# Moving copies, additions and one division between engines in a fused attention and FFN kernel

## The chip, the cores and the metric

The kernel runs on one core of one Trainium2 chip, as one launch. The metric is the device time of the program in microseconds (us). Its engines are named as the profile names them: PE is TensorE (matrix products and transposes), DVE is VectorE, ACT is ScalarE, POOL is GpSimd, SP is SyncE (here only DMA issue). Each engine works through its own queue in order, and waits on semaphores for the others.

## The reference

`x` is 2 x 2048 rows of 512, f32; the encoder output `enc` is 2 x 128 rows of 512. There are 16 heads of width 32, and 128 keys.

```python
q = layernorm(x) @ wq + bq;  k = enc @ wk + bk;  v = enc @ wv + bv
score = q k^T / sqrt(32) * mask           # per head
score = where(score == 0, -1e9, score)
context = softmax(score) @ v              # over 128 keys
x = x + context @ wo + bo
n = layernorm(x)
y = real(ifft(fft(n) @ (w_re + i w_im)))  # over the 512 columns
out = x + y + bias
```

## The kernel before

The 4096 rows are cut into 8 groups of four tiles of 128 rows. Tile (i, t) is tile t of group i. Everything that belongs to one group is spread over about three groups of time: while the softmax of group i runs, the queries of group i+1 are made, the rows of group i+2 are normalized and transposed, and the output projection and the FFN of group i-1 run.

**Softmax of a tile.** `begin` (L760) lets PE make the scores of 16 heads (32 products, L326) into two PSUM tiles of two banks each, one for each half of the heads. Each half then goes through four steps. `masked` (L345, DVE) multiplies scores by the mask and puts them into SBUF. `maxima` (L352, L354, L355, all DVE) marks zeros, takes the row maxima of 8 heads and scales them. `exponentials` (L361, ACT) is 8 ACTIVATE instructions with a sum each. `divided` is a reciprocal on DVE (L373) and a multiplication by it, on GpSimd unless another engine is given (L374).

**Transposed weights.** `transposed_weights(i, t, first, end, eng, banks)` (L380) lets PE transpose the divided weights of four heads into one PSUM bank (L399), once for each g from first to end, and copies each bank to SBUF (tensor `pt`), on ACT (L390) or on the engine `eng` (L388). Four such copies, g = 0 to 3, make up a tile. With `banks`, all transposes come first and go into the banks given.

**PSUM.** There are eight banks: two tiles of two banks for scores (`ps_sc`, tag sc), two single banks for transposes (`ps_tp`, tag tp) and two for matrix chains (`ps_mm`, tag mm). In each pool the buffers are used in turn: a third request waits until the first one has been read out. `transpose_rows` (L185) transposes four 128 x 128 blocks (L194) and copies them out (L196 on ACT, L198 otherwise); its argument `spare` picks the pool. `chain` (L204) is four accumulating products (L210), in the mm pool or, with `spare=True`, in the tp pool. Both a chain of queries (`Queries`), of the projection (`Project`) and of the FFN (`Ffn`) has a `pe` and an `evict` part, and `between` puts transposes in the middle of a chain.

**Other helpers.** `relative` (L234) subtracts its first column from a tile of rows: one instruction on DVE or GpSimd (L244), two on ACT (L241, L242). `query_statistics` and `query_norm` (L227) normalize it; `query_transposes` transposes it (tensor `xnT`, on ACT). `output_bias` (L435) adds `bo` to the four residual tiles of a group, on GpSimd (L439), before `Project.evict` (L460) adds the projection. `ffn_statistics`, `ffn_norm` (L227 on DVE, then the FFN's bias on GpSimd, L479) and `ffn_transposes` prepare the FFN; `Ffn.evict` (L524) adds and stores. `Mirrored` and `First` make the 512 x 512 matrix of the FFN (`m_ffn`) out of its Fourier weights, during group 0.

**Order.** The kernel is built under a manual schedule: the order of the calls is the order of each engine's queue. Group 0 and the first two tiles of group 1 (L880 to L1027) are written out by hand, as are tiles 1 to 3 of the last group (L1144 on). In between, `slot` (L765) places the work of one tile: its hooks `pool`, `early`, `mid_a`, `on_a`, `on_m`, `mid_b`, `mid_c`, `on_b`, `end` and `on_c` take extra calls, and `carried` holds calls put off to the next slot, where they run right after the first `masked`. `turned` names the tile whose weights are transposed in the slot, which is the tile before.

Of the kernel before, what the change touches and what calls it, by code (L numbers as in the profile page):

```python
# [14 lines left out]
P = 128  # L15
# [7 lines left out]
def kernel(  # L23
# [210 lines left out]
    def relative(i, t, eng):  # L234


        xt = rows[i][t]
        d = work.tile([P, D], FP, tag="rel", bufs=4, name=f"rel_{i}_{t}")
        if eng is nc.scalar:
            less = small.tile([P, 1], FP, tag="less", name=f"less_{i}_{t}")  # L240
            nc.scalar.mul(less, xt[:, 0:1], -1.0)  # L241
            nc.scalar.activation(d, xt, AF.Identity, bias=less)  # L242
        else:
            eng.tensor_scalar(d, xt, xt[:, 0:1], None, ALU.subtract)  # L244
        rels.setdefault(i, []).append(d)
# [39 lines left out]
    class Queries:  # L285


        def __init__(self, i, g, first=0, spare=False):
            self.i, self.g, self.first, self.spare = i, g, first, spare
# [87 lines left out]

    pts = {}

    def transposed_weights(i, t, first, end, eng=None, banks=None):  # L380
        if t == 0 and first == 0:
            pts[i] = [big_tile("pt", 6, f"pt_{i}_{g}") for g in range(NC)]
        ws = weights[i, t]

        def copy(g, ps):
            dst = pts[i][g][:, :, t * P : (t + 1) * P]
            if eng:
                eng.tensor_copy(dst, ps)  # L388
            else:
                nc.scalar.copy(dst, ps)  # L390

        for g in range(first, end):
            ps = (
                banks[g]
                if banks
                else ps_tp.tile([P, NR, P], FP, tag="tp", name=f"tpw_{i}_{t}_{g}")
            )
            for r in range(NR):
                nc.tensor.transpose(  # L399
                    ps[:, r, :], ws[r // 2].w[:, (r % 2) * NC + g, :], ident  # L400
                )
            if not banks:
                copy(g, ps)
        if banks:
            for g in range(first, end):
                copy(g, banks[g])

# [24 lines left out]
            else:  # L432
                eng.tensor_copy(cT[:, g, :], ps)

    def output_bias(i):  # L435

        xs = groups[i]
        for t in range(TG):
            nc.gpsimd.tensor_tensor(xs[:, t, :], xs[:, t, :], bo, ALU.add)  # L439

    fstats = {}
# [42 lines left out]
        transpose_rows(nTs[i, t], norms.pop((i, t)), f"f{i}_{t}", eng, spare)  # L484

    class Ffn:
        def __init__(self, i, t):
            self.i, self.t = i, t

        def pe(self, between=()):  # L490
            nT = nTs.pop((self.i, self.t))
            self.ps = chain(
                f"y_{self.i}_{self.t}",
                lambda c: nT[:, c, :],
                lambda c: m_ffn[:, c, :],
                between=between,
            )

        def in_halves(self):
# [208 lines left out]
    def load_first_rows(name, pieces):  # L708

        rows = small.tile([NC, P], FP, tag="rows0", bufs=2, name=name)  # L710
        for k, piece in enumerate(pieces):
            nc.sync.dma_start(rows[k : k + 1, :], piece)
        return rows
# [242 lines left out]
    h[1].first()  # L956
    w[0].exponentials()
    w[1].masked()
    transposed_weights(0, 2, 0, HC, nc.vector)
    h[1].second()  # L960
    h[2].pe()
    h[2].evict()
# [3 lines left out]
    h[3].first()  # L966
    w[1].maxima()
    w[0].divided()
    relative(3, 0, nc.gpsimd)
    h[2].second()  # L970
    h[3].second()
    load_residual(0)
    rows_m = load_first_rows("rows_m", [x.lhs(HC)[0:1, :] for x in m])
    w[1].exponentials()
    run(q[0])
    transposed_weights(0, 2, HC, NC, nc.vector)
    w[1].divided()
    relative(3, 1, nc.gpsimd)

    load_mask(2)  # L980
    w = begin(1, 0)
# [1 line left out]
    m[0].pe()  # L983
    add = first_rows("add_m", rows_m)
    m[0].evict(add[:, 0:1])
    w[0].maxima()
    relative(3, 2, nc.gpsimd)
    relative(3, 3, nc.gpsimd)
    m[1].pe()
    m[1].evict(add[:, 1:2])  # L990
    transposed_weights(0, 3, 0, HC)
    w[0].exponentials()
    w[1].masked()
    w[1].maxima()
# [13 lines left out]
    context(0, 0, NC, nc.scalar, True)  # L1008
    m[3].pe()
    m[3].evict(add[:, 3:4])  # L1010
    output_bias(0)
    w[0].maxima()
    q[2].pe()
    w[0].exponentials()
    w[1].masked()
    q[2].evict()
    free = ps_sc.tile([P, 2, NC, K], FP, tag="sc", name="tpw_1_0")
    transposed_weights(1, 0, 0, HC, nc.vector, [free[:, g] for g in range(HC)])
    transposed_weights(1, 0, HC, NC)
    w[1].maxima()  # L1020
    q[3].pe()
# [2 lines left out]
    query_norm(3, 0)  # L1024
    query_norm(3, 1)
    w[0].divided()
    carried.append(w[1].divided)  # L1027


    for i in range(1, last - 1):  # L1030
        p, pp, n, nn = i - 1, i - 2, i + 1, i + 2
        q = [Queries(n, g) for g in range(NC)]
        q_nn = Queries(nn, 0)
        o = [Project(p, t) for t in range(TG)]
        f_p = Ffn(p, 0)
        if i > 1:
            load_rows(nn)
            load_mask(n)
            load_residual(p)
            f_pp = [Ffn(pp, t) for t in range(TG)]  # L1040
            slot(
                i,
                0,
                [f_pp[1], f_pp[2], q[1]],
                turned=(p, TG - 1),
                early=[(ffn_transposes, pp, 2)],
                pool=[(relative, nn, t, nc.gpsimd) for t in range(TG)],
                on_b=[(ffn_norm, pp, 3), (query_statistics, nn, 0, 2)],
                on_c=[(query_statistics, nn, 2, TG)],
            )  # L1050
            slot(
                i,
                1,
                [q[2], q[3], f_pp[3]],
                turned=(i, 0),
                early=[(context, p, 0, NC, nc.scalar, True), (ffn_transposes, pp, 3)],
                pool=[(output_bias, p)],
                on_b=[(query_norm, nn, 0), (query_norm, nn, 1)],
            )
        slot(  # L1060
            i,
            2,
            o[:3],
            turned=(i, 1),
            early=[(query_transposes, nn, 0), (query_transposes, nn, 1)],
            on_a=[(ffn_statistics, p, 0)],
            on_m=[(ffn_norm, p, 0), (query_norm, nn, 2), (query_norm, nn, 3)],
            on_c=[(ffn_statistics, p, 1)],
            end=[(ffn_transposes, p, 0)],
        )  # L1070
        slot(
            i,
            3,
            [o[3], f_p, q_nn],
            turned=(i, 2),
            early=[(query_transposes, nn, 2), (query_transposes, nn, 3)],
            on_a=[(ffn_statistics, p, 2)],
            on_b=[(ffn_norm, p, 1), (ffn_statistics, p, 3)],
            on_c=[(ffn_norm, p, 2)],
            end=[(ffn_transposes, p, 1)],  # L1080
        )
# [41 lines left out]
        pool=[(ffn_norm, p, 0)],  # L1123
        mid_a=[(ffn_transposes, p, 0, nc.scalar, ps_sc)],
        on_a=[(ffn_statistics, p, 1)],
        on_b=[(ffn_norm, p, 1), (ffn_statistics, p, 2), (ffn_statistics, p, 3)],
        end=[(ffn_transposes, p, 1)],
    )
    i, p, pp = last, last - 1, last - 2
    o = [Project(p, t) for t in range(TG)]  # L1130
    f = f_p
    f_p = [Ffn(p, t) for t in range(TG)]
    slot(
        i,
# [60 lines left out]
    w[0].exponentials()  # L1195
    w[1].masked()
    f_p[0].evict()
    f_p[1].pe(between=[(ffn_transposes, p, 2, nc.vector)])
    ffn_norm(p, 3)
    w[1].maxima()  # L1200
    transposed_weights(i, 2, HC, NC)
# [79 lines left out]
```

## Time and profile before

| | |
|---|---|
| median of 3 runs | 530.56 us (530.26 to 532.3) |
| the profiled execution | 530.73 us, of which the instructions span 528.6 |
| PE busy | 519.5 us, 98% |
| DVE busy | 433.5 us, 82% |
| ACT busy | 339.0 us, 64% |
| POOL busy | 335.0 us, 63% |
| PE clock granted | full speed |

The profile is one execution, taken by the hardware profiler. Its first part gives each engine's busy time with its share of the span. Rows of waits name who waited for whom, with the total, the count and the longest wait in us. The chain that ended last is followed back from the last instruction, at each step to what released it. Rows of a timeline give start, duration, engine, line, operation, output and input, shapes, and a count where equal neighbours are merged; in square brackets stands the idle time before, with what ended it. Releasers are inferred from semaphores. L12 is line 12 of the kernel before.

### The profile page before, as it was taken

The numbers are of one execution on the slowest core, as the hardware profiler recorded it, in microseconds if no ns is written. First come the engines' busy times: TensorE is split into PE (matmuls) and PEld (weight loads), VectorE is DVE, ScalarE is ACT, GpSimd is POOL, SyncE is SP. The second block draws the span as 40 slices with busy tenths as digits, with TensorE's granted clock in tenths as the row PEclk, the third lists the DMA queues.
The fourth block names the chain that finished last, engine by engine and source line by source line (L and its number), as shares of the span: only waits on it lengthen the run. The fifth ranks groups of instructions, "written<-read, shape, count | busy, mean of one in ns | idle before, by whom it ended". The sixth has DMA issues, their size and how long they took to land.

```text
span 528.6 us, 8816 instructions
## 1 busy us (share of the span) xinstructions
PE 519.5 (98%) x3028; PEld 294.8 (56%) x3028; DVE 433.5 (82%) x618; ACT 339.0 (64%) x1290; POOL 335.0 (63%) x275
## 2 busy tenths in 40 slices
PE   8999999989999999999999999999999999999997
PEld 7756675545545555455545555455545555455444
DVE  4789898989887988889887998889876898998351
ACT  3367878486667776666677676666686677766210
POOL 2779379955993559635894459635764466756450
PEclk9999999999999999999999999999999999999999
DMA  8962030000600033000610015000312001201002
GB/s 317 383 236 79 1 100 3 0 2 0 221 21 20 1 115 125 1 20 1 200 41 1 20 60 180 1 22 0 120 42 65 35 1 61 100 0 52 29 0 81
DMA packets 22892, 36.49 MB, mean 69 GB/s; under 512 B 2104, under 2 KB 7488, under 8 KB 22848
## 3 DMA queue, kind: packets, MB, share of 16 engines
q1 hardware_dynamic: 22160, 34.75, 19.1%
q10 hardware_dynamic: 688, 1.18, 0.6%
q8 instruction: 24, 0.39, 0.3%
q14 instruction: 20, 0.16, 0.1%
HBM read 27.53 MB, written 8.39 MB: 68 GB/s over the span
## 4 chain that ended last, share of the span: by engine, by line
PE 77%; DVE 14%; ACT 5%; POOL 1%; issue 1%; DMA 1%; SPq 0%; ACTq 0%; POOLq 0%; DVEq 0%
PE q L210 17%; PE y L210 16%; PE o L210 16%; PE tpw L399 8%; PE sc L326 5%; PE c L423 5%; ACT w L361 4%; DVE w L352 3%; DVE nmax L354 3%; PE tp_a L194 3%; DVE w L345 3%; PE tp_f L194 2%; PE k L568 1%; PE v L210 1%; DVE norm_f L227 1%
## 5 line engine op out<-in xcount | busy, mean ns | idle before, releaser
L361 ACT ACTIVATE w<-w,nmax 128x128 f32<-128x128 f32 x512 | 198.3, 395 | 21.0 <-DVE nmax L355 17.0
L374 POOL TENSOR_TENSOR w<-w,rden 128x1024 f32<-128x1024 f32 x62 | 118.8, 1920 | 71.7 <-DVE rden L373 56.3
L210 PE MATMUL o<-wo,cT 128*128 128x512 f32 x256 | 115.3, 594 | 0.0
L210 PE MATMUL y<-m_ffn,nT 128*128 128x512 f32 x248 | 112.1, 594 | 0.5 <-DVE x L524 0.5
L210 PE MATMUL q<-xnT,wq 128*128 128x512 f32 (+1 forms) x256 | 111.6, 580 | 0.0
L361 ACT ACTIVATION_READ_ACCUMULATOR w<-w,nmax 128x1 f32 x512 | 99.3, 194 | 0.0
L390 ACT COPY pt<-tpw 128x512 f32<-128x512 f32 x114 | 60.9, 586 | 55.6 <-PE tpw L399 55.4
L352 DVE SCALAR_TENSOR_TENSOR w<-w 128x1024 f32<-128x1024 f32 x64 | 87.9, 1373 | 0.8
L345 DVE TENSOR_TENSOR w<-sc,mask 128x1024 f32<-128x1024 f32 x64 | 77.4, 1211 | 8.1 <-PE sc L326 7.4
L354 DVE TENSOR_REDUCE nmax<-w 128x8 f32<-128x1024 f32 x64 | 78.1, 1220 | 2.2
L399 PEld LDWEIGHTS tpw<-ident,w 128*128 128x128 f32 x496 | 57.7, 141 | 32.4 <-issue 28.1
L210 PEld LDWEIGHTS o<-wo,cT 128*128 128x128 f32 x256 | 46.2, 190 | 47.5 <-issue 46.2
L210 PEld LDWEIGHTS q<-xnT,wq 128*128 128x128 f32 x256 | 46.4, 190 | 44.6 <-issue 40.2
L210 PEld LDWEIGHTS y<-m_ffn,nT 128*128 128x128 f32 x248 | 44.5, 190 | 45.2 <-issue 44.2
L399 PE MATMUL tpw<-ident,w 128*128 128x128 f32 x496 | 64.9, 273 | 1.2 <-POOL w L374 1.0
L479 POOL TENSOR_TENSOR x<-x,bf 128x512 f32<-128x512 f32 x32 | 50.4, 1573 | 23.5 <-DVE norm_f L227 23.5
L223 POOL TENSOR_SCALAR rstd_f<-mv_f 128x1 f32<-128x1 f32 x32 | 17.8, 557 | 62.7 <-DVE mv_f L220 62.7
L373 DVE RECIPROCAL rden<-den 128x8 f32<-128x8 f32 x64 | 12.6, 198 | 41.2 <-ACT w L361 41.0
L439 POOL TENSOR_TENSOR x<-x,bo 128x512 f32<-128x512 f32 x32 | 45.6, 1452 | 0.0
L244 POOL TENSOR_SCALAR rel<-rows 128x512 f32<-128x512 f32 x25 | 43.7, 1760 | 1.1 <-PE tp_a L194 1.1
L326 PEld LDWEIGHTS sc<-kT,qT 32*128 32x128 f32 x1024 | 31.5, 186 | 14.2 <-issue 11.8
L196 ACT COPY nT<-tp_f 128x512 f32<-128x512 f32 x29 | 16.9, 583 | 34.1 <-PE tp_f L194 34.0
(92 smaller groups left out, 553.9 us busy)
## 6 DMA issues: line engine op xcount, KB each, us to landing
rows<-in_x_dram SPq DMA_DIRECT2D x32, 256.0 KB, 5.1
x<-in_x_dram SPq DMA_DIRECT2D x32, 256.0 KB, 4.8
out_dram<-x SPq DMA_DIRECT2D x31, 256.0 KB, 2.0
mask<-in_mask_Bx1xSxS_fk_dram SPq DMA_DIRECT2D x8, 256.0 KB, 4.7
wk<-in_L_xattn_wk_w_dram ACTq DMA_DIRECT2D x2, 512.0 KB, 6.7
wq<-in_L_xattn_wq_w_dram SPq DMA_DIRECT2D x1, 1024.0 KB, 7.1
wr<-n_L_ffn_w_freq_real_dram SPq DMA_DIRECT2D x2, 512.0 KB
wi<-n_L_ffn_w_freq_imag_dram SPq DMA_DIRECT2D x2, 512.0 KB, 8.7
```

Of the source, the lines that this page charges most:

```text
L210: nc.tensor.matmul(ps, lhs(c), rhs(c), start=(c == 0), stop=(c == NC - 1))
L244: eng.tensor_scalar(d, xt, xt[:, 0:1], None, ALU.subtract)
L326: nc.tensor.matmul(sc[r // 2][:, r % 2, g, :], qTs[i][rows, g, t * P : (t + 1) * P], kT[rows, g, b * K : (b + 1) * K], start=True, stop=True,)
L345: nc.vector.tensor_tensor(self.w, self.sc.rearrange("p r g k -> p (r g) k"), self.mrow, ALU.mult)
L352: nc.vector.scalar_tensor_tensor(w, w, 0.0, w, ALU.is_equal, ALU.subtract)
L354: nc.vector.tensor_reduce(self.nmax, w, AX.X, ALU.min)
L361: nc.scalar.activation(w[:, h, :], w[:, h, :], AF.Exp, bias=self.nmax[:, h : h + 1], scale=-UNIT, accum_out=self.den[:, h : h + 1],)
L374: eng.tensor_tensor(w, w, rden.unsqueeze(2).to_broadcast([P, HH, K]), ALU.mult)
L390: nc.scalar.copy(dst, ps)
L399: nc.tensor.transpose(ps[:, r, :], ws[r // 2].w[:, (r % 2) * NC + g, :], ident)
L439: nc.gpsimd.tensor_tensor(xs[:, t, :], xs[:, t, :], bo, ALU.add)
L479: nc.gpsimd.tensor_tensor(xt, xt, bf, ALU.add)
```

## The change

Five parts of the hand-written order move, and two calls change their PSUM pool:

- The four weight copies of tile (0, 2) and the first two of tile (1, 0) go from DVE to ACT. The first two of (0, 2) are put off (new argument `later`) and issued just before the exponentials of the second half of (0, 3); the first two of (1, 0) are issued before the eviction of `q[2]`.
- The subtractions of the four tiles of group 3 come later; tiles 0 and 3 are subtracted by ACT, 1 and 2 stay on GpSimd.
- `output_bias(0)`, four additions on GpSimd, leaves tile (1, 1): its first two go to the `pool` hook of the slot of tile (1, 2), the other two to that slot's `mid_a`.
- The second half of tile (1, 1), whose division is carried into the slot of (1, 2), is divided on DVE.
- In the second last group's last slot one FFN normalization moves from `on_b` to `on_m`. The last FFN chain of group 5 (`f[3]`, run during tile 1 of the last group) takes a transpose bank, and the FFN transposes of tile 2 of group 6 go into a score tile.

```diff
-    def transposed_weights(i, t, first, end, eng=None, banks=None):
+    def transposed_weights(i, t, first, end, eng=None, banks=None, later=None):
...
-            if not banks:
+            if later is not None:
+                later.append((copy, g, ps))
+            elif not banks:
                 copy(g, ps)
-        if banks:
+        if banks and later is None:
...
-    def output_bias(i):
+    def output_bias(i, first=0, end=TG):
         xs = groups[i]
-        for t in range(TG):
+        for t in range(first, end):
             nc.gpsimd.tensor_tensor(xs[:, t, :], xs[:, t, :], bo, ALU.add)
...
     class Ffn:
-        def __init__(self, i, t):
-            self.i, self.t = i, t
+        def __init__(self, i, t, spare=False):
+            self.i, self.t, self.spare = i, t, spare
...
                 between=between,
+                spare=self.spare,
...
     w[1].masked()
-    transposed_weights(0, 2, 0, HC, nc.vector)
+    copies = []
+    transposed_weights(0, 2, 0, HC, later=copies)
     h[1].second()
...
     w[0].divided()
-    relative(3, 0, nc.gpsimd)
     h[2].second()
     h[3].second()
     load_residual(0)
     rows_m = load_first_rows("rows_m", [x.lhs(HC)[0:1, :] for x in m])
+    call(copies)
     w[1].exponentials()
     run(q[0])
-    transposed_weights(0, 2, HC, NC, nc.vector)
+    transposed_weights(0, 2, HC, NC)
     w[1].divided()
-    relative(3, 1, nc.gpsimd)
...
     m[0].evict(add[:, 0:1])
+    relative(3, 0, nc.scalar)
     w[0].maxima()
-    relative(3, 2, nc.gpsimd)
-    relative(3, 3, nc.gpsimd)
+    relative(3, 1, nc.gpsimd)
     m[1].pe()
     m[1].evict(add[:, 1:2])
+    relative(3, 2, nc.gpsimd)
     transposed_weights(0, 3, 0, HC)
+    relative(3, 3, nc.scalar)
     w[0].exponentials()
...
     m[3].evict(add[:, 3:4])
-    output_bias(0)
     w[0].maxima()
     q[2].pe()
     w[0].exponentials()
     w[1].masked()
+    free = ps_sc.tile([P, 2, NC, K], FP, tag="sc", name="tpw_1_0")
+    transposed_weights(1, 0, 0, HC, banks=[free[:, g] for g in range(HC)])
     q[2].evict()
-    free = ps_sc.tile([P, 2, NC, K], FP, tag="sc", name="tpw_1_0")
-    transposed_weights(1, 0, 0, HC, nc.vector, [free[:, g] for g in range(HC)])
     transposed_weights(1, 0, HC, NC)
...
-    carried.append(w[1].divided)
+    carried.append(lambda half=w[1]: half.divided(nc.vector))
...
             early=[(query_transposes, nn, 0), (query_transposes, nn, 1)],
+            pool=[(output_bias, p, 0, HC)] if i == 1 else [],
+            mid_a=[(output_bias, p, HC, TG)] if i == 1 else [],
...
         on_a=[(ffn_statistics, p, 1)],
-        on_b=[(ffn_norm, p, 1), (ffn_statistics, p, 2), (ffn_statistics, p, 3)],
+        on_m=[(ffn_norm, p, 1)],
+        on_b=[(ffn_statistics, p, 2), (ffn_statistics, p, 3)],
...
     f = f_p
+    f[TG - 1].spare = True
...
-    f_p[1].pe(between=[(ffn_transposes, p, 2, nc.vector)])
+    f_p[1].pe(between=[(ffn_transposes, p, 2, nc.vector, ps_sc)])
```

## The prediction

> **What bounds the kernel now.** I read the page's first part, then TensorE's own waits, the chain that ended last, and the timelines of the engines around each wait.
>
> ```profile
> PE 519.5 (98%) x3028; PEld 294.8 (56%) x3028; DVE 433.5 (82%) x618; ACT 339.0 (64%) x1290; POOL 335.0 (63%) x275
> ```
>
> TensorE (PE) is busy for 519.5 of 528.6 us, and the clock row is full throughout. Some 5.2 us of its idle time lie in the first 20 us and at the very end, where the change does nothing. What it can win is in these five waits (total, count, longest):
>
> ```profile
> PE tp_a L194 <- DVE rel L227: 1.8, 1, 1.8
> ...
> PE tpw L399 <- POOL w L374: 1.0, 1, 1.0
> PE y L210 <- DVE x L524: 0.5, 1, 0.5
> ...
> PE tp_f L194 <- DVE norm_f L227: 0.3, 1, 0.3
> ...
> PE tpw L399 <- DVE nT L198: 0.2, 1, 0.2
> ```
>
> They make 3.8 us, at 104.4, 111.0, 444.6, 431.7 and 482.2 us. The first two end the start-up stage; the others belong to the last two groups. Between 112 and 400 us the chain is TensorE alone, so whatever is won at 104 to 112 us is carried through. Before and after that it is a softmax chain (DVE, ACT, POOL):
>
> ```profile
> 101.26 2.01 DVE w L352
> 103.29 1.23 DVE nmax L354
> 104.55 1.10 DVE nmax L355
> 105.67 3.20 ACT w L361 x16
> 109.24 2.71 POOL w L374
> 111.99 0.88 PE tpw L399 x6
> ```
>
> Why VectorE is late is in its timeline (start, duration) and in GpSimd's:
>
> ```profile
> 99.99 1.27 DVE L388 COPY pt<-tpw 128x512 f32<-128x512 f32 x2
> 101.19 2.07 DVE L352 SCALAR_TENSOR_TENSOR w<-w 128x1024 f32<-128x1024 f32 x1
> 103.29 1.22 DVE L354 TENSOR_REDUCE nmax<-w 128x8 f32<-128x1024 f32 x1
> 104.55 1.09 DVE L355 TENSOR_SCALAR nmax<-nmax 128x8 f32<-128x8 f32 x1
> ```
>
> ```profile
> 94.03 1.90 POOL L374 TENSOR_TENSOR w<-w,rden 128x1024 f32<-128x1024 f32 x1
> ...
> 99.68 5.93 POOL L439 TENSOR_TENSOR x<-x,bo 128x512 f32<-128x512 f32 x4
> ```
>
> L352 takes 1.17 us with GpSimd quiet (109.01 us) and L355 0.17. Here they take 2.07 and 1.09: they end when a bias addition (L439) has ended plus their own length, and the additions are stretched in turn. The two engines alternate on SBUF operands; PSUM readers (L345, L388) and the reduction are not stretched. I use this throughout: an L352, L355, L227 or L374 on VectorE waits for the GpSimd instruction in progress, and GpSimd for it.
>
> **The start-up stage, part by part.**
>
> Copies of tile (0,2). VectorE loses twice 1.2 us. ScalarE gets two pairs at 0.96 us a pair (the pair at 87.43 us is followed at 88.39). The first pair stands before the exponentials, where ScalarE idled 1.36 us (72.26 to 73.62); the second after the query eviction, ahead of an idle 1.69 us before L720. No free bank is wanted sooner: the first pair ends near 73.1, the next transposes start at 74.8. Cost nothing; without those idle times 1.9 us.
>
> A rule speaks against this: the Trainium skill, "ScalarE: Activation LUTs", "Rules for kernel authors", wants simple arithmetic on VectorE, which it calls up to about 3 times faster (bf16). Applied here, six copies would take some 6 x 3 x 0.68 = 12 us of ScalarE (estimate), more than its idle time in this stage, and make it the bound. The rows for this very copy, f32 out of PSUM, say 676 ns on VectorE (L388) and 586 on ScalarE (L390). I take the rows.
>
> Two subtractions. ScalarE has this pair of instructions at the start (L241 187 ns, L242 722 ns; 0.85 us from pair to pair). One lands in its idle 1.00 us before the second m_ffn eviction (81.0 us), the other in the idle 0.97 before the exponentials at 83.73. GpSimd loses two of 1.62 us (median). "GPSIMD Engine Reference", "Engine selection", calls single-input work there roughly line-rate: 512 elements at its 1.2 GHz are 0.43 us (estimate), and then the move would be a loss of 0.4 us each. The row decides; by either the path sees only this: the division of tile (0,3) no longer queues behind a subtraction, it ends near 79.3 instead of 81.1, and the transposes at 80.80, stretched to 1.27 us against 1.04 elsewhere, lose 0.2. ScalarE is then full from 79 to 91 us, so the exponentials of (1,0) come only 0.2 us earlier although VectorE is over 1 us ahead.
>
> Bias, and copies of (1,0). From 93.1 us VectorE runs unstretched: the division at 94.03 moves to 91.7, so L352 at 94.53 (2.47) becomes 1.2; the maxima of (1,1), first half, come at 97.1 instead of 98.9. Then 1.2 of copies, 0.9 at L352 and 0.9 at L355 go too: second half at 100.8 instead of 105.6, the two normalizations (L227, 0.45 each) by 101.7. TensorE wants them at 104.2. The first wait, 1.79, is gone. ScalarE: exponentials 97.1 to 100.2, copies to 101.2, q eviction (0.58, queued behind the copies; its bank is wanted only at 105) to 101.7, copies to 102.7, exponentials to 105.8 (before: 108.8). The score bank is free at 101.2, wanted at 103.1.
>
> Division of (1,1) by VectorE. L374 takes 1.22 us there (row at 461.04). It waits for the exponentials, until 105.85, and holds back all of VectorE's queue. GpSimd has the other half until 103.75 and then four additions of 1.24 each: the second ends at 106.25, so the division ends at 107.4. TensorE reaches these transposes at 108.6. The second wait, 1.02, is gone: TensorE is 1.79 + 1.02 + 0.2 = 3.0 us ahead.
>
> What is late next: tile (1,2). L352 stands behind the division and then behind the third bias addition (107.4 to 108.65); its maxima come at 111.1 instead of 111.96, 0.85 ahead where TensorE is 3.0 ahead. The second half follows (maxima 117.2 before, 116.35 now), then 3.1 of exponentials and 0.55 of the copy of nT, 120.05. That copy frees the transpose bank of the fourth query transpose:
>
> ```profile
> 121.08 0.59 ACT L196 COPY nT<-tp_f 128x512 f32<-128x512 f32 x1 [0.16 <-PE tp_f L194]
> ```
>
> ```profile
> 122.08 1.09 PE L194 MATMUL tp_a<-ident,rel 128*128 128x128 f32 x8
> ```
>
> The fourth starts halfway, 122.65; 3.0 ahead it would want the bank at 119.65 and gets it at 120.1. A new wait of 0.45; net 2.55. Both ends: 3.0 if the bias never meets the softmax; 1.3 if one more addition (1.24) gets in first. I take 2.55. In the next slot ScalarE waited 3.2 us for TensorE (127.08), which absorbs the rest.
>
> **The last two groups.** The normalization moved up to `on_m` (called at L824) then stands before the division and the evictions, at 429.3, with GpSimd idle: the wait of 0.25 goes, TensorE and VectorE both 0.25 ahead at the scores of 432.5. The FFN chain in a transpose bank (copied out at 443.3) starts at 444.5 instead of 445.1: 0.55. The transposes into a score bank free the next ones: 0.20. But this stretch is a chain of VectorE and ScalarE: after the FFN result L352 waits for GpSimd's division anyway (ends 449.85), so the maxima move by 0.25 only; at 460.8 the reciprocal comes 0.2 earlier still, with TensorE's earlier o. Later VectorE's copy of nT at 486.02 to 486.66 just precedes its chain at 486.78. So TensorE gives back what it is ahead of VectorE: net 0.45, bounds 0.2 and 1.0.
>
> **The sum.** 2.55 + 0.45 = 3.0. The profiled execution took 530.73 (span 528.6): 527.7. Against the median, 530.56: 527.6, or 0.57% less. About 0.5%, 2.65 us, is what this kernel's measurement tells from no change: the bound is 527.9, so the sign is surer than the class.
>
> **The rivals.**
>
> All waits go (0.12). Nothing new appears: 3.0 + 1.0, 526.6. For it: ScalarE and VectorE have idle time. Against it: the 0.45 at the fourth transpose and the softmax chain at the end.
>
> The bias takes back what it gave (0.27). Moved one tile on, the additions meet the division and L352 of (1,2), and one more gets in, or the end gives nothing: gain 1.3 to 2.3, 528.3 to 529.3, no measurable change. For it: the stretched L352 at 101.19.
>
> ScalarE becomes the bound (0.06), on the other side. It takes 6 x 0.48 + 2 x 0.87 = 4.6 us, all ahead of exponentials. If no idle time absorbed any of it, the division of (1,1) would follow at 113.5 (108.9 + 4.6), the fourth transpose at 125.5 instead of 122.65, 2.9 late; less 0.45 at the end: 533.0, and with one addition between, 534. It eats the gain of this stage once the maxima of (1,2) come 1.7 us later than before. Against it: 1.36, 1.69, 1.00, 0.97 and 3.48 us of ScalarE idle in the very places.
>
> That an edit doesn't do its part would show as one of the five waits remaining; this lies in the ranges.
>
> **The numbers.** My forecast has 0.55, with 526.9 to 528.4 as its own range; four fifths of it lie under 527.9. Faster: 0.45 + 0.12 = 0.57. Same: 0.10 + 0.27 = 0.37. Slower 0.06. Predicted 527.6; range 526.6 (all waits gone) to 529.4 (the bias case).
>
> **What would show it.** Right: no wait of tp_a on L227 at 104 nor of tpw on GpSimd at 111; ScalarE's copies before the exponentials at 73; L374 once on VectorE near 106 to 107.4, L352 after it stretched by a bias addition; TensorE waiting some 0.5 us for a bank (ScalarE's nT copy) near 120; TensorE's work of 112 to 400 us shifted by 2.5; no wait on L524 near 442, but one of some 0.5 on VectorE after 480. Wrong: exponentials of (1,0) later than 83.7, maxima of (1,2) at 112 or later, or a wait at 104 still there.

## The result, and the profile after

The changed kernel takes 528.35 us (median; 527.83 to 529.5) against 530.69 us of the kernel before (530.26 to 532.3) on the same chip. The ratio is 0.9952, with a 95% interval of 0.9937 to 0.9966: 0.48% less. The whole interval lies under 1, so the gain is certain; whether it exceeds the 0.5% that the prediction took for the least that can be told from no change, the interval leaves open. The profiled execution took 528.42 us, with a span of 526.2.

The page after, engines' busy times and the chain that ended last by engine:

```profile
PE 520.0 (99%) x3028; PEld 295.1 (56%) x3028; DVE 429.8 (82%) x613; ACT 343.2 (65%) x1300; POOL 329.9 (63%) x272
...
PE 84%; DVE 8%; ACT 6%; issue 1%; POOL 0%; ACTq 0%; POOLq 0%; DVEq 0%
```

The same row of the page before:

```profile
PE 77%; DVE 14%; ACT 5%; POOL 1%; issue 1%; DMA 1%; SPq 0%; ACTq 0%; POOLq 0%; DVEq 0%
```

TensorE is as busy as before in a shorter span, and the chain runs over VectorE for 8% of it instead of 14%. TensorE's own waits after (total, count, longest) leave, apart from those of the first 20 us, only these two:

```profile
PE tp_a L194 <- ACT nT L196: 0.7, 1, 0.7
...
PE y L210 <- DVE nT L198: 0.2, 1, 0.2
```

All five waits of before are gone. One of 0.7 us has come in, at the place and with the cause that the prediction named, and one of 0.2. (In the kernel after, the lines of the helpers below L400 stand some three lines further down: L439 is L442, L460 is L463, L479 is L482, L524 is L528.)

**The first two waits.** VectorE's timeline after, where L352 took 2.07 us and L355 1.09 before:

```profile
98.13 1.23 DVE L352 SCALAR_TENSOR_TENSOR w<-w 128x1024 f32<-128x1024 f32 x1
99.40 1.22 DVE L354 TENSOR_REDUCE nmax<-w 128x8 f32<-128x1024 f32 x1
100.65 0.17 DVE L355 TENSOR_SCALAR nmax<-nmax 128x8 f32<-128x8 f32 x1
100.73 1.00 DVE L227 TENSOR_SCALAR rel<-rel,mv,rstd 128x512 f32<-128x512 f32 x2
```

The first of the two normalizations ends near 101.3 us. TensorE starts to read it at 104.16:

```profile
104.16 1.09 PE L194 MATMUL tp_a<-ident,rel 128*128 128x128 f32 x8
```

The wait of 1.79 us has gone, and there are 2.9 us to spare. What this surplus means is the subject of the experiments.

**The new wait.** GpSimd, VectorE, ScalarE and TensorE after, one timeline each:

```profile
103.84 6.92 POOL L442 TENSOR_TENSOR x<-x,bo 128x512 f32<-128x512 f32 x4
```

```profile
106.05 1.38 DVE L374 TENSOR_TENSOR w<-w,rden 128x1024 f32<-128x1024 f32 x1
107.35 2.28 DVE L352 SCALAR_TENSOR_TENSOR w<-w 128x1024 f32<-128x1024 f32 x1
```

```profile
119.54 0.56 ACT L196 COPY nT<-tp_f 128x512 f32<-128x512 f32 x1
```

```profile
120.16 0.66 PE L194 MATMUL tp_a<-ident,rel 128*128 128x128 f32 x4 [0.73 <-ACT nT L196]
```

The division that moved to VectorE runs once, at 106.05. L352 of tile (1,2) right behind it takes 2.28 us instead of 1.2, because a bias addition holds it up; twelve microseconds later ScalarE's copy of nT is late, and the fourth query transpose waits for the bank that it frees. Of the four additions the first two take 1.28 us each, the last two, which meet VectorE's operations, 2.25.

**How far ahead TensorE is.** I compare the start of the same matrix product in two traces, and call the difference TensorE's lead. Each execution has its own shift from the first loads (up to 1.2 us) and from waits of 0.2 us at 79 to 84 us (the run below that has only the last two groups changed loses 0.47 us there against the profile of before, and is the same kernel up to that point). So I count the lead from the transposes of the weights of (1,0) on (they start at 97.99 us before). From there the change is 1.87 us ahead at the first projection (107.16 before), 3.10 at the first FFN transposes (120.45), 2.15 at the first FFN product (127.32), 1.98 at the second FFN transposes (135.07), and it stays there until 426 us; at the last FFN transposes (517.89) it is 2.13. At 97.99 us it was 0.22 us ahead already: 0.27 won at 81 us (0.24 in the runs below) and 0.15 from the first loads, less 0.20 lost at 79 us. The total is 2.35, and the span is 2.4 us shorter. So the first two waits paid 1.87 and 1.23, the new one took 0.95 back, another 0.17 went at 132 us, and the last two groups gave 0.15.

### The profile page after: what moved, and what is told of

Same layout as the page of the kernel before. It is cut to its first block, busy times and chain, and to the rows that moved or that the text cites. A ratio compares the mean times of both kernels' runs of the same rounds, so it can differ in the third digit from the quotient of the medians.

```text
span 526.2 us, 8813 instructions
## 1 busy us (share of the span) xinstructions
PE 520.0 (99%) x3028; PEld 295.1 (56%) x3028; DVE 429.8 (82%) x613; ACT 343.2 (65%) x1300; POOL 329.9 (63%) x272
## 4 chain that ended last, share of the span: by engine, by line
PE 84%; DVE 8%; ACT 6%; issue 1%; POOL 0%; ACTq 0%; POOLq 0%; DVEq 0%
PE y L210 18%; PE q L210 18%; PE o L210 16%; PE tpw L400 8%; PE sc L326 6%; ACT w L361 5%; PE c L426 4%; PE tp_a L194 3%; PE tp_f L194 3%; DVE w L352 2%; DVE nmax L354 2%; PE half L672 1%; PE k L572 1%; PE v L210 1%; DVE w L345 1%; ACT pt L391 1%
## 5 line engine op out<-in xcount | busy, mean ns | idle before, releaser
L374 POOL TENSOR_TENSOR w<-w,rden 128x1024 f32<-128x1024 f32 x61 | 116.1, 1908 | 73.6 <-DVE rden L373 57.0
L391 ACT COPY pt<-tpw 128x512 f32<-128x512 f32 x120 | 64.0, 586 | 54.8 <-PE tpw L400 54.7
L352 DVE SCALAR_TENSOR_TENSOR w<-w 128x1024 f32<-128x1024 f32 x64 | 88.3, 1380 | 0.9
L345 DVE TENSOR_TENSOR w<-sc,mask 128x1024 f32<-128x1024 f32 x64 | 77.5, 1212 | 10.1 <-PE sc L326 9.4
L354 DVE TENSOR_REDUCE nmax<-w 128x8 f32<-128x1024 f32 x64 | 78.1, 1220 | 2.2
L400 PEld LDWEIGHTS tpw<-ident,w 128*128 128x128 f32 x496 | 57.7, 141 | 30.5 <-issue 28.4
L482 POOL TENSOR_TENSOR x<-x,bf 128x512 f32<-128x512 f32 x32 | 50.4, 1574 | 24.7 <-DVE norm_f L227 24.7
L400 PE MATMUL tpw<-ident,w 128*128 128x128 f32 x496 | 64.3, 273 | 0.0
L223 POOL TENSOR_SCALAR rstd_f<-mv_f 128x1 f32<-128x1 f32 x32 | 19.0, 594 | 61.1 <-DVE mv_f L220 61.1
L442 POOL TENSOR_TENSOR x<-x,bo 128x512 f32<-128x512 f32 x32 | 47.3, 1509 | 0.0
L244 POOL TENSOR_SCALAR rel<-rows 128x512 f32<-128x512 f32 x23 | 38.5, 1688 | 1.2 <-DMA rows<-in_x_dram 1.2
```

The lines of the kernel that those rows point to most:

```text
L345: nc.vector.tensor_tensor(self.w, self.sc.rearrange("p r g k -> p (r g) k"), self.mrow, ALU.mult)
L352: nc.vector.scalar_tensor_tensor(w, w, 0.0, w, ALU.is_equal, ALU.subtract)
L354: nc.vector.tensor_reduce(self.nmax, w, AX.X, ALU.min)
L374: eng.tensor_tensor(w, w, rden.unsqueeze(2).to_broadcast([P, HH, K]), ALU.mult)
L400: nc.tensor.transpose(ps[:, r, :], ws[r // 2].w[:, (r % 2) * NC + g, :], ident)
L482: nc.gpsimd.tensor_tensor(xt, xt, bf, ALU.add)
```

## The experiments

All diffs are against the changed kernel. Ratios are to the kernel before on the same chip, where it took 532.31 us beside the first four runs, 530.75 beside the next four and 531.0 beside the last. The figures in us of the first four expectations are spans on the scale of the profiles above (528.6 before, 526.2 after). "Lead" is TensorE's, counted as above. The intervals of most of these ratios overlap, so differences between the runs rest on the leads, one trace for each run; two traces of the changed kernel give the same leads to 0.02 us.

### Either half of the change alone

The start-up stage alone (`e1_start_only`) takes back the three edits of the last two groups:

```diff
-        on_m=[(ffn_norm, p, 1)],
-        on_b=[(ffn_statistics, p, 2), (ffn_statistics, p, 3)],
+        on_b=[(ffn_norm, p, 1), (ffn_statistics, p, 2), (ffn_statistics, p, 3)],
...
-    f[TG - 1].spare = True
...
-    f_p[1].pe(between=[(ffn_transposes, p, 2, nc.vector, ps_sc)])
+    f_p[1].pe(between=[(ffn_transposes, p, 2, nc.vector)])
```

> The changed kernel with its three edits in the last two groups undone. My account: TensorE is 2.2 us ahead of the kernel before from 128 to 400 us, as in the full change, and the three waits of the end return (0.25 on L227, 0.55 on the FFN result, 0.2 on the nT copy); but the end is a chain of VectorE and ScalarE, in which the full change gained only 0.2, so the span is 526.4, 0.2 over the full change. Rival, the waits add up: their 1.0 us is lost, span 527.2.

The last two groups alone (`e2_tail_only`) is the kernel before with only these three edits.

> The kernel before with only the three edits in the last two groups. My account: the three waits go and others of TensorE on VectorE's nT copies come, span 528.4, 0.2 under before (no measurable change). Rival, the waits add up: 527.6, 1.0 under before.

The first measured 529.49 us, ratio 0.9948 (0.9933 to 0.9963); the second 532.03 us, 0.9999 (0.999 to 1.0008). The leads at the end are 1.94 and 0.16 us. So the waits do not add up as they stand in the table of waits: the three edits of the last two groups take away 1.0 us of waits and win 0.16. The start-up stage makes the whole of what can be measured. (Its ratio is worth 2.8 us and its lead 1.94: the 0.47 us that the other run lost at 79 to 84 us is in the kernel before on this chip too, if its executions there are like that run's, and the 0.24 us at 81 are not in the lead.)

### Without the moved additions, and with the division on GpSimd

`e3_no_bias` leaves out the additions of `bo` to group 0, which is a part of the computation; its time tells what the additions cost and nothing else.

```diff
-            pool=[(output_bias, p, 0, HC)] if i == 1 else [],
-            mid_a=[(output_bias, p, HC, TG)] if i == 1 else [],
```

> The changed kernel without the four bias additions of group 0, so the first 512 rows lack the output bias. If the additions delay the softmax of tile (1,2), its L352 at 107 takes 1.2 instead of 2.3 us, the maxima come 1.3 earlier (109.6), and TensorE's wait of 0.73 on ScalarE's nT copy near 120 is gone: span 525.5. If the wait is ScalarE's own order and load, it stays at 0.7, and the span at 526.2.

Measured: 528.31 us, ratio 0.9927 (0.991 to 0.9943). The wait at the fourth query transpose is gone, the lead stays at 3.09 at 127 us and ends at 3.16, against 2.13 for the change. The additions cost 1.0 us where the change puts them.

`e4_pool_division` leaves the additions where the change has them and gives the division of (1,1) back to GpSimd:

```diff
-    carried.append(lambda half=w[1]: half.divided(nc.vector))
+    carried.append(w[1].divided)
```

> The changed kernel with the division of the second half of tile (1,1) left on GpSimd, before the bias additions. If the division on VectorE is what removed the second wait, TensorE waits 1 us or more for it again, at 108.5, and the span is 527. My account: with the bias behind it GpSimd starts it at 105.9 and ends it between 107.8 and 109.0, so that wait is 0 to 0.5; L352 of tile (1,2) then starts at 105.9 instead of 107.35, its maxima are 2 us earlier, and the wait near 120 is gone: span 525.6 to 526.2.

Measured: 529.02 us, ratio 0.9941 (0.9926 to 0.9956), lead at the end 2.50 us. The small gain lies in what I had put (a span 0 to 0.6 us shorter); the rival, a wait of 1 us or more, did not come. GpSimd's, VectorE's and TensorE's timelines of this run:

```profile
107.17 2.70 POOL L374 TENSOR_TENSOR w<-w,rden 128x1024 f32<-128x1024 f32 x1 [2.31 <-DVE rden L373]
109.84 5.95 POOL L442 TENSOR_TENSOR x<-x,bo 128x512 f32<-128x512 f32 x4
```

```profile
106.95 1.17 DVE L352 SCALAR_TENSOR_TENSOR w<-w 128x1024 f32<-128x1024 f32 x1
```

```profile
109.46 1.34 PE L400 MATMUL tpw<-ident,w 128*128 128x128 f32 x8
```

The division now stands ahead of the additions on GpSimd, so they start 5 us later against TensorE (this execution is 0.94 us behind the other), L352 slips in unstretched, and the wait near 120 us is gone. Of the second wait 0.3 us is left: the division ends at 109.87, and the transposes that read it take 1.34 us instead of 1.04. Another 0.33 goes at the second FFN transposes. So 0.9 of the 1.23 us of the second wait did not need the move of the division to VectorE, and with the additions where they are, the move costs 0.4 us. What it is worth with the additions out of the way was not run.

### The additions back in their old place

`e5_bias_back`:

```diff
     m[3].evict(add[:, 3:4])
+    output_bias(0)
     w[0].maxima()
...
-            pool=[(output_bias, p, 0, HC)] if i == 1 else [],
-            mid_a=[(output_bias, p, HC, TG)] if i == 1 else [],
```

> The changed kernel, but all four additions of bo of group 0 stand again where they stood before the change, behind the fourth FFN weight chain in tile (1,1). My theory (the first wait, 1.79 us, came from VectorE's SBUF operations being held up by GpSimd's divisions and additions at 94 to 103 us): the additions run at 97 to 102 us, meet the second difference of (1,1) at 98.1 us, and bring back 0.5 to 1.2 us of the first wait; in exchange the 0.73 us wait at the fourth query transpose is gone. Net 0 to 0.5 us behind or ahead of the changed kernel's 0.9952 of before: ratio 0.994 to 0.997. Rival (the wait came from the weight copies on VectorE, and the moved additions only cost): the first wait does not come back at all, the 0.73 us is won, ratio 0.9935 to 0.994.

Measured: 527.67 us, ratio 0.9934 (0.9911 to 0.9956), the lead at the end 3.04 us. This is the rival's number, and my theory was half wrong: no part of the first wait came back. VectorE, GpSimd and TensorE of this run:

```profile
98.43 2.32 DVE L352 SCALAR_TENSOR_TENSOR w<-w 128x1024 f32<-128x1024 f32 x1
...
102.04 1.10 DVE L355 TENSOR_SCALAR nmax<-nmax 128x8 f32<-128x8 f32 x1
103.06 0.99 DVE L227 TENSOR_SCALAR rel<-rel,mv,rstd 128x512 f32<-128x512 f32 x2
```

```profile
97.16 5.95 POOL L442 TENSOR_TENSOR x<-x,bo 128x512 f32<-128x512 f32 x4
```

```profile
104.46 1.09 PE L194 MATMUL tp_a<-ident,rel 128*128 128x128 f32 x8
```

The stretching is there as foretold: L352 takes 2.32 us, L355 1.10, and the normalizations come 2 us later. That alternation is what the Trainium skill, "SBUF — State Buffer", section "SBUF: two separate sides", describes as an exclusive lock held for a whole instruction; the trace agrees with it: the second addition ends 1.24 us after L352 has started, L352 ends 1.08 us after that, and L354 and L345 keep their 1.22. But there were 2.9 us to spare, and 0.9 are left, so TensorE does not wait. The wait that the moved additions were to help remove is gone with the additions unmoved.

### What did remove the first wait

`e6_copies_back` puts the four copies of (0,2) back on VectorE:

```diff
-    copies = []
-    transposed_weights(0, 2, 0, HC, later=copies)
+    transposed_weights(0, 2, 0, HC, nc.vector)
...
-    call(copies)
...
-    transposed_weights(0, 2, HC, NC)
+    transposed_weights(0, 2, HC, NC, nc.vector)
```

> The changed kernel, but the four weight copies of tile (0,2) are on VectorE again, where they were before the change. My theory: VectorE waits for the scores of (1,1) at 93.1 us anyway (in both traces it starts its mask addition there the moment TensorE has them), so 2.5 us more of copies before 80 us end in its idle time at 85 to 91 us: the waits at 104 and 112 us stay away, at most 0.2 to 0.5 us is lost around 80 us, ratio 0.9952 to 0.9960. Rival (the copies are a real part of the gain, as the few words of the change have it): 1.3 us or more of the first wait comes back, ratio 0.9975 to 0.998.

Measured: 528.68 us, ratio 0.9962 (0.9945 to 0.9978). From 98 us on its leads are those of the changed kernel to 0.03 us, and end at the same 2.13. What is missing is the 0.24 us that the changed kernel wins at 81 us. The copies of (0,2) pay for nothing else: In the changed kernel VectorE is rid of 2.5 us of work and idles all the longer: 4.4 us instead of 2.4 between 66 and 93 us, of it 2.26 instead of 1.77 ahead of the reciprocal at 91.4. It waits there for ScalarE's exponentials, and not for the scores at 93 us, as I had put it.

The remaining two runs start from the kernel with the additions back, which has little slack, so that a lost share of the gain must show. `e9_bias_subs_back` also gives the subtractions back to GpSimd at their old places:

```diff
     w[0].divided()
+    relative(3, 0, nc.gpsimd)
...
     w[1].divided()
+    relative(3, 1, nc.gpsimd)
...
-    relative(3, 0, nc.scalar)
     w[0].maxima()
-    relative(3, 1, nc.gpsimd)
+    relative(3, 2, nc.gpsimd)
+    relative(3, 3, nc.gpsimd)
...
-    relative(3, 2, nc.gpsimd)
...
-    relative(3, 3, nc.scalar)
```

> The kernel of the run with the bias additions put back, and the two subtractions of query group 3 back on GpSimd as well, at their old places. Left of the change in the start-up stage: the weight copies of (0,2) and (1,0) on ScalarE and the division on VectorE. In the run with the bias back the first norm of query group 3 ends near 103.5 us and TensorE wants it at 104.5 us, 0.9 us of slack. My theory (the subtractions push GpSimd's divisions into the differences of (1,1), which stretches L352 to 2.5 us and the small L355 after it): 1.7 us later on VectorE, so a wait of 0.5 to 1.1 us at the first query transpose, ratio 0.0010 to 0.0020 above that run's 0.9934. Rival (the subtractions are worth what their own time is, hidden in GpSimd's idle time): no wait, the same ratio.

Measured: 528.31 us, ratio 0.9951 (0.9936 to 0.9966). It is 0.0017 above the run with the additions alone put back (0.9 us), as expected; the intervals overlap, but the traces have as much: 0.6 us less lead at the end, and some 0.4 at 81 us. TensorE's waits, and what GpSimd and VectorE did ahead of the first of them:

```profile
PE tp_a L194 <- DVE rel L227: 0.4, 1, 0.4
PE tpw L400 <- POOL w L374: 0.2, 1, 0.2
```

```profile
92.81 1.90 POOL L374 TENSOR_TENSOR w<-w,rden 128x1024 f32<-128x1024 f32 x1
```

```profile
93.41 2.38 DVE L352 SCALAR_TENSOR_TENSOR w<-w 128x1024 f32<-128x1024 f32 x1
...
98.88 1.94 DVE L352 SCALAR_TENSOR_TENSOR w<-w 128x1024 f32<-128x1024 f32 x1
```

The second wait, at 81 us, is for a division that queues behind a subtraction again. With two subtractions more, GpSimd's division of (1,0) meets the first L352 of (1,1), which takes 2.38 us instead of 1.22. The wait that comes back, 0.43 us, is a little less than the 0.5 to 1.1 that I had put, because I had left out what ScalarE gets in return: without the subtractions its exponentials are 1.2 us earlier (the reciprocal on VectorE that waits for them stands at 90.50 us, with the additions alone put back at 91.67).

`e10_bias_copies_back` leaves the subtractions on ScalarE and gives all six copies back to VectorE, those of (0,2) as above and those of (1,0):

```diff
-    transposed_weights(1, 0, 0, HC, banks=[free[:, g] for g in range(HC)])
     q[2].evict()
+    transposed_weights(1, 0, 0, HC, nc.vector, [free[:, g] for g in range(HC)])
```

> The kernel of the run with the bias additions put back, and all the weight copies, of (0,2) and of the first half of (1,0), back on VectorE. Left of the change in the start-up stage: two subtractions on ScalarE and the division on VectorE. My theory: of these copies only the two of (1,0), 1.2 us, stand in the stretch of VectorE that ends at the first query transpose; against 0.9 us of slack they bring back a wait of 0.2 to 0.6 us, ratio 0.0003 to 0.0012 above 0.9934. Rival (the copies are the heart of the change): the first wait comes back nearly whole, 1.3 to 1.8 us, ratio 0.9960 to 0.9970.

Measured: 527.93 us, ratio 0.9946 (0.9933 to 0.996). I had put a wait of 0.2 to 0.6 us at the first query transpose, and there is none. The copies push L352 behind the middle of the additions, where it takes 1.67 us instead of 2.32, and L355 behind their end, where it takes 0.17 instead of 1.10. So of their 1.2 us only 0.35 arrive at the normalizations (103.24 us against 103.06, and this execution is shifted by 0.17 the other way):

```profile
98.99 1.29 DVE L389 COPY pt<-tpw 128x512 f32<-128x512 f32 x2 [0.70 <-PE tpw L400]
100.19 1.67 DVE L352 SCALAR_TENSOR_TENSOR w<-w 128x1024 f32<-128x1024 f32 x1
...
103.16 0.17 DVE L355 TENSOR_SCALAR nmax<-nmax 128x8 f32<-128x8 f32 x1
```

The lead drops later, by 0.36 us at the fourth query transpose, and ends at 2.72. So the six copies together are worth 0.3 us there and 0.2 us at 81 us.

These two runs say more about the first wait. The division of (1,1) runs behind it and has no part in it. With the additions and all copies back, only the moved subtractions are left ahead of it, and the lead at the projection is the full 1.86: they remove the first wait alone. With the additions and the subtractions back, only the copies are left, and they remove 1.37 of it. The edits overlap: each takes VectorE away from the same wait, so their worths do not add up.

### Better places for the additions, and both together

`e7_bias_spread` puts the first addition behind the third FFN weight chain, the second behind the fourth, and leaves two in the slot of (1,2):

```diff
     m[2].evict(add[:, 2:3])
+    output_bias(0, 0, 1)
...
     m[3].evict(add[:, 3:4])
+    output_bias(0, 1, HC)
...
-            pool=[(output_bias, p, 0, HC)] if i == 1 else [],
-            mid_a=[(output_bias, p, HC, TG)] if i == 1 else [],
+            pool=[(output_bias, p, HC, TG)] if i == 1 else [],
```

> The changed kernel, but the four additions of bo of group 0 are spread: tile 0 behind the third FFN weight chain (GpSimd idle from 90.4 to 91.7 us, VectorE idle too), tile 1 behind the fourth (GpSimd idle from 96.9 us, VectorE busy with a mask addition that reads PSUM), tiles 2 and 3 at the start of tile (1,2), where all four are now. My theory (the 0.73 us wait at the fourth query transpose comes from the third and fourth addition holding up the difference of (1,2), 2.28 us instead of 1.2): with two additions it ends by 109 us, that wait is gone and little comes in its place; 0.6 to 0.9 us under the changed kernel, ratio 0.9935 to 0.9941. Rival (the wait comes from the division that now runs on VectorE, whatever GpSimd does): no gain, ratio 0.995 to 0.9955, with 0.5 to 0.7 us of the wait left.

Measured: 527.71 us, ratio 0.9934 (0.9916 to 0.9951). GpSimd's and VectorE's timelines:

```profile
104.61 2.50 POOL L442 TENSOR_TENSOR x<-x,bo 128x512 f32<-128x512 f32 x2
```

```profile
106.83 1.37 DVE L374 TENSOR_TENSOR w<-w,rden 128x1024 f32<-128x1024 f32 x1
108.12 1.21 DVE L352 SCALAR_TENSOR_TENSOR w<-w 128x1024 f32<-128x1024 f32 x1
```

The division is on VectorE as in the change, and L352 behind it is unstretched; the new wait is gone. So the division on VectorE does not make this wait by itself: it takes the third and fourth addition right behind it. (With the division on GpSimd and all four additions behind it, the wait was gone too.) The lead is 3.09 at 127 us and 3.20 at the end.

`e8_late_bf` concerns the next to last group. The normalization that the change moves up brings an addition on GpSimd along (`ffn_norm` issues L227 on VectorE and L482 on GpSimd). Here this addition alone is put off to the next slot (a third argument of `ffn_norm` leaves it out). GpSimd and VectorE in the changed kernel:

```profile
427.72 1.27 POOL L482 TENSOR_TENSOR x<-x,bf 128x512 f32<-128x512 f32 x1 [1.26 <-DVE norm_f L227]
428.95 1.89 POOL L374 TENSOR_TENSOR w<-w,rden 128x1024 f32<-128x1024 f32 x1
...
432.50 1.90 POOL L374 TENSOR_TENSOR w<-w,rden 128x1024 f32<-128x1024 f32 x1
```

```profile
432.81 1.87 DVE L227 TENSOR_SCALAR norm_f<-x,mv_f,rstd_f 128x512 f32<-128x512 f32 x1
```

```diff
+    def ffn_bias(i, t):
+        xt = groups[i][:, t, :]
+        nc.gpsimd.tensor_tensor(xt, xt, bf, ALU.add)
...
-        on_m=[(ffn_norm, p, 1)],
+        on_m=[(ffn_norm, p, 1, False)],
...
-        pool=[(ffn_norm, pp, 2)],
+        pool=[(ffn_norm, pp, 2), (ffn_bias, pp, 1)],
```

> The changed kernel, but in the next to last group the addition of bf that came along with the earlier norm (GpSimd, 427.7 to 429.0 us, ahead of the division) is put off behind GpSimd's later work. My theory (that addition held the division back, which then held up the norm at 432.8 us, 1.87 us instead of 0.54, and with it the transpose at 434.8 us): the norm ends about 0.8 us earlier, TensorE keeps 0.3 us at 434.8 us and ends 0.2 to 0.6 us earlier, ratio 0.9941 to 0.9948. Rival (the end is set by VectorE's chain behind it whatever the norm does): the transpose is earlier, the end is not, ratio 0.9952.

Measured: 528.03 us, ratio 0.9942 (0.9923 to 0.9961). The same two rows there:

```profile
431.17 1.90 POOL L374 TENSOR_TENSOR w<-w,rden 128x1024 f32<-128x1024 f32 x1
```

```profile
432.55 0.80 DVE L227 TENSOR_SCALAR norm_f<-x,mv_f,rstd_f 128x512 f32<-128x512 f32 x1
```

The normalization takes 0.80 us instead of 1.87. Its transposes start 0.28 us earlier against TensorE's own schedule, and at the end 0.14 of that is left (lead 2.27 against 2.13), so both sides had something. The other half goes at the projection near 451 us, which waits for VectorE's copy of cT behind an L352 and an L355 that GpSimd holds up: there the lead falls by 0.46 us in this run and by 0.28 in the changed kernel. The ratio itself cannot tell 0.14 us.

`e11_spread_late` joins the two, and `e12_after_again` is the changed kernel beside it:

> The two alterations that paid, together: the additions of bo of group 0 spread over three places, and the early addition of bf in the next to last group put off. My theory (they act at 120 us and at 434 us and do not touch each other): 0.9 and 0.15 us under the changed kernel, ratio 0.9930 to 0.9936, TensorE with no wait between 60 and 480 us except two of 0.2 us. Rival (the gain of the first is lost again in the last two groups, where VectorE sets the pace): ratio 0.9945 to 0.9952.

> The changed kernel again, to stand beside the other three on the same chip: 0.9945 to 0.9955, with the wait of 0.7 us at the fourth query transpose.

Measured: 527.00 us, ratio 0.9929 (0.9916 to 0.9941), against 528.52 us, 0.9957 (0.9944 to 0.9969), for the changed kernel on the same chip. The two intervals do not meet, and this version beats both kernels: 4.0 us under before, 1.5 under the change. TensorE keeps its lead of 3.10 us from 120 us on and ends with 3.37. TensorE's waits in it behind the first 20 us:

```profile
PE o L210 <- DVE cT L436: 0.2, 1, 0.2
...
PE y L210 <- DVE nT L198: 0.2, 1, 0.2
```

The leads of all runs, in us:

| kernel | ratio | projection, 107 us | FFN transposes, 120 | FFN product, 127 | FFN transposes, 135 | last, 518 |
|---|---|---|---|---|---|---|
| the change | 0.9952 | 1.87 | 3.10 | 2.15 | 1.98 | 2.13 |
| start-up stage alone | 0.9948 | 1.86 | 3.10 | 2.14 | 1.98 | 1.94 |
| last two groups alone | 0.9999 | -0.01 | -0.02 | -0.03 | -0.02 | 0.16 |
| no additions | 0.9927 | 1.86 | 3.10 | 3.09 | 3.10 | 3.16 |
| division on GpSimd | 0.9941 | 1.86 | 2.79 | 2.79 | 2.46 | 2.50 |
| additions back | 0.9934 | 1.87 | 3.10 | 3.08 | 2.92 | 3.04 |
| copies of (0,2) back | 0.9962 | 1.86 | 3.10 | 2.12 | 1.95 | 2.13 |
| additions spread | 0.9934 | 1.86 | 3.10 | 3.09 | 3.06 | 3.20 |
| late bf | 0.9942 | 1.86 | 3.10 | 2.16 | 1.98 | 2.27 |
| additions and subtractions back | 0.9951 | 1.37 | 2.61 | 2.45 | 2.28 | 2.44 |
| additions and all copies back | 0.9946 | 1.86 | 3.09 | 2.73 | 2.56 | 2.72 |
| spread and late bf | 0.9929 | 1.87 | 3.10 | 3.10 | 3.08 | 3.37 |
| the change again | 0.9957 | 1.86 | 3.10 | 2.16 | 1.99 | 2.15 |

## Why the prediction was right, and where not

The time, 528.35 us, is 0.75 above the forecast of 527.6 and inside its range; it lies at the upper edge of the likeliest case's own range (526.9 to 528.4) and at the lower edge of the bias rival's (528.3 to 529.3). The forecast gave 0.57 to a gain of more than 0.5%, and the measured 0.48% is just under that line.

In TensorE's lead, the forecast's 3.0 us were 3.0 won by 112 us, less 0.45 at 120, and 0.45 in the last two groups. Measured: 3.3, less 0.95, less 0.17 at 132 us, and 0.15. The 0.3 more that was won was lost again in the wait, so it did not help the number. What is missing is 0.2 at 120, 0.17 at 132 and 0.3 at the end.

**Right, to a tenth or two.** The maxima of (1,1) end at 96.97 and 100.82 us (forecast 97.1 and 100.8), the exponentials at 105.8 (105.8), the maxima of (1,2) at 111.09 (111.1), the copy of nT at 120.10 (120.05). The first two waits are gone, and TensorE waits near 120 us for ScalarE's copy of nT. Some 0.24 us are won at 81 us (forecast 0.2); putting back either the copies of (0,2) or the subtractions loses them. Both rules of the skill that were turned down were rightly turned down: the copies take 586 ns each on ScalarE after the change too, which is 65% busy and holds 6% of the chain; moving two subtractions away from GpSimd was a gain, since putting them back cost 0.6 us of lead and some 0.4 at 81 us.

**"A new wait of 0.45; net 2.55" was too small on one side.** The wait cost 0.95 us of lead. Of the difference, 0.3 is that TensorE came 3.3 us ahead of before (3.10 and the 0.22 that it had at 97.99 us), and not 3.0: the second wait, 1.02 in the table of waits, was worth 1.23. The bank came when forecast, so the more TensorE is ahead, the longer it waits. The rest, 0.22 us beyond the 0.73 that the row shows, is the break in a run of eight transposes: two runs of four take 0.66 us each, one of eight 1.09.

**"In the next slot ScalarE waited 3.2 us for TensorE, which absorbs the rest" failed** by 0.17 us. At 132 us the second FFN transposes wait for a normalization that GpSimd's division holds up. I had looked for slack on ScalarE alone.

**"The last two groups: net 0.45" measured 0.15.** The step that failed is "with GpSimd idle: the wait of 0.25 goes, TensorE and VectorE both 0.25 ahead". I counted the normalization that moves and not the addition on GpSimd that it issues with it. That addition goes ahead of the division, which then meets the next normalization (1.87 us), and TensorE gives 0.29 of its lead back at 434.8 us. Put off, it yields 0.14. The other half of the missing 0.3 is given back to VectorE's chain: 0.28 at 451 us, 0.19 at 471 and 0.35 behind 480, where the row of waits has 0.2. That TensorE gives back what it is ahead of VectorE was foreseen, though not how much.

**The credit for the first wait was given wrongly.** The sum was right, but it let the moved additions and the copies share in the removal. With the additions back at their old place the wait stays away, with 0.9 us to spare, and the subtractions alone suffice. I never asked by how much the forecast overshot: normalizations by 101.7 where TensorE wants them at 104.2 stand in the prediction, 2.5 us of slack, and the additions' own terms there are 0.9 and 0.9, together 1.8 (2.3 measured). The prediction had all it takes to see that this edit gives nothing at 104 us and takes at 120.

The rival "the bias takes back what it gave" had the right edit in its name, though the additions gave nothing and cost 0.9 to 1.0 us. Of its two ways, "one more gets in" did not happen: the maxima of (1,2) came when the main case had them, behind the third addition. "The end gives nothing" nearly did. "All waits go" is refuted by the wait at 120 us, and "ScalarE becomes the bound" by the leads and the chain.

What stays open: whether the moved additions alone would have removed the first wait, and what the copies of (1,0) do without those of (0,2). Neither was run. For the 1.87 us there is no one division among the edits, because they overlap.

## What to carry to other kernels

When several edits aim at one wait, work out by how much the wait is overshot, and leave out the edit whose share is smaller than the surplus, above all if it puts its work somewhere else. In this kernel an addition on GpSimd is not free because GpSimd is idle: it costs where VectorE runs one of L352, L355, L227 or L374 in the same microsecond, so place it beside VectorE's PSUM readers, its reductions or its idle time. And when a call is moved, move in your sum every instruction that it issues, on every engine.

## What was not expected of the hardware

A small instruction pays the whole price of the alternation: L355 works on 128 x 8 elements and takes 0.17 us alone, but 1.10 us when an addition of 1.24 us is in progress (102.04 us with the additions back), nearly as much extra as L352 with 128 times the data (1.22 to 2.32). And pushing VectorE's work back can shorten it: with 1.2 us of copies put ahead of it, L352 took 1.67 us instead of 2.32 and L355 0.17 instead of 1.10, and the chain behind them arrived 0.35 us later, not 1.2.
